# Gathers of a graph-attention kernel: leave to start at three instructions of a step instead of eleven

## The chip, the cores and the metric

The kernel runs on one core of one Trainium2 chip. The metric is the device time of one execution in microseconds (us), the median of several runs. Names of engines: PE is the TensorE (matmuls; PEld its weight loads), DVE the VectorE, ACT the ScalarE, POOL the GpSimd, SP the SyncE, which here only issues DMAs.

## The reference, cut to what matters

A graph layer with attention over 100,000 edges, 3,125 nodes, 5 edge types (relations) and 8 heads of 16 channels. The edges are sorted by destination.

```python
for r in range(5):
    mask = edge_types == r
    q = einsum('eh,khd->ekd', x[dst], W_Q[r])
    k = einsum('eh,khd->ekd', x[src], W_K[r])
    v = einsum('eh,khd->ekd', x[src], W_V[r])
    logits = (q * k).sum(-1) / 4 + attn_bias[r]
    # softmax over the edges of one destination and one relation
    attn = segment_softmax(where(mask, logits, -1e9), dst)
    out += segment_sum(attn * v, dst)
out = out @ out_proj_w.T + out_proj_b
h = layernorm(out + x) * gamma + beta
result = layernorm(x + h)
```

## The kernel before

**Tables first.** For every node and relation the kernel computes a row of keys and values (256 float32) and writes it to a table in device memory, `kv_d`; the queries go to a second table, `q_d`. This preamble takes about the first 105 us of the profile.

**Then steps.** The edges are taken 128 at a time (a tile), four tiles to a group and three groups to a step `k`, 66 steps in all (the first and the last have two groups). For each tile POOL issues one indirect DMA, a *gather* (L836), which fetches the 128 rows of `kv_d` that the tile's edges need. In 63 of the steps one of the twelve tiles is made by matmuls instead (`early_rows`, L1060, from rows of x gathered in the preamble at L371), so that a step has eleven gathers: 719 gathers at L836 in all, and 63 at L371.

**Where gathers land.** There are four slots of twelve tiles: three in the tile `kv_early`, one in `kv_late`; step `k` uses slot `k % 4` (`place`, L804). A gather may write a slot once the step that used it four steps earlier has been read for the last time, by `weigh` (L1118).

**One step.** DVE multiplies the gathered keys by the queries (`products`, L933), sums over channels (`logits`, L991), and adds the relation's mask (L966). PE turns the result (L1023). DVE then divides the sums of step `k-2` by their denominators (`norm`, L1169 its first instruction, L1173 its last), PE spreads the queries of step `k+1` (`spread_q`, L911, 36 matmuls into `qe`), DVE multiplies the values of step `k-1` by their weights (`weigh`, L1118), runs two scans that give the running maxima (L1073, L1077) and subtracts (L1087); ACT takes the exponential (L1095), PE turns it (L1102), and ACT copies the weights (`weights`, L1112), almost the last thing of the step. ACT also makes the matrices (L1131, L1135) by which PE sums edges into nodes (L1152, `sums`).

**What orders the gathers.** All engines run in the order in which the code writes their instructions; there is no scheduler. POOL's queue in the steps holds nothing but gathers. `gather(leave, n)` issues the next `n` of them and makes each wait for one instruction of another engine, its *leave* (`behind`, L154). `point(k, j, leave)` is called eleven times in a step, `j` from 0 to 10, and computes how many gathers should have been issued by then: those of the steps up to `k + (j+1)/11 + lead`, where `lead` falls evenly from 3.0 steps at the start (`KV_LEAD`) to 2.0 at the end (`KV_LOW`). As a step has about eleven gathers, each point issues about one. Besides its leave each gather waits for the landing of the gather eight places before it (eight semaphores, DMASW0 to DMASW7, are used in turn), and for whatever its slot needs, where the leave doesn't already cover that.

The points 6 to 10 of step `k-1` are written in the code of step `k`; the leaves of one round are, in the order of the code: `products(k)`, `weighted` (the L1112 copy of step `k-1`), `logits(k)`, the two ends of `norm(k-2)` (L1169, L1173), `weigh(k-1)` (L1118), `kept` (the last matmul of `spread_q(k+1)`, L911), the two scans (L1073, L1077), the masks `spot(k+2)` (L720) and `placed` (L1135).

Of the kernel before, what the change touches and what calls it, by code (L numbers as in the profile page):

```python
# [146 lines left out]
def windowed_path(  # L147
# [6 lines left out]
    def behind(gather, other):  # L154
        if other is not None:
            tc.add_manual_dep(
                gather.ins,
                other.ins.name,
                mybir.DependencyInfo(mybir.DependencyClass.Sync, mybir.DependencyReason.DATA),
                reason="leave",  # L160
            )
# [646 lines left out]
    def runs(a, b):  # L808
        out_ = []
        for q in range(a, b):  # L810
            k = AT[q // T][0]
            kv, at = place(k)
            at += q - T * G0[k]
            if out_ and out_[-1][0] is kv and out_[-1][2] == at:
                out_[-1][2] += 1
            else:
                out_.append([kv, at, at + 1])
        return out_
# [13 lines left out]
    def gather(leave=None, n=1):  # L832
        for q in sum(tiles, [])[len(issued) :][: max(n, 0)]:
            ((kv, at, _),) = runs(q, q + 1)
            behind(
                nc.gpsimd.indirect_dma_start(  # L836
                    out=kv[:, at, :], out_offset=None, in_=kv_d[:, :],
                    in_offset=bass.IndirectOffsetOnAxis(
                        ap=idx[:, q % T, q // T : q // T + 1], axis=0
                    ),  # L840
                ),
                leave,
            )
            issued.append(q)

    def point(k, j, leave):
        at = k + (j + 1) / POINTS
        at += KV_LEAD - (KV_LEAD - KV_LOW) * min(max(at / (NST - 3), 0.0), 1.0)
        whole = min(int(at), NST)
        n = sum(len(t) for t in tiles[:whole])  # L850
        if whole < NST:
            n += int((at - whole) * len(tiles[whole]) + 1e-6)
        gather(leave, n - len(issued))
# [493 lines left out]
    q_at = {k: b for b, k in q_from.items()}  # L1347

    gather(n=len(tiles[0]))
    assert len(marks) >= len(tiles[1]) + len(tiles[2])  # L1350
    for leave in marks[: len(tiles[1]) + len(tiles[2])]:
# [23 lines left out]
    for k in range(NST - 1):  # L1375
# [24 lines left out]
        if k < NST - 2:  # L1400
            point(k - 1, 6, products(k))
            point(k - 1, 7, weighted)
            point(k - 1, 8, logits(k))
            closed_lanes(k)
        else:
            places(G0[k])
            for g in range(G3 - 1):
                piece(k, g)
            made, summed = piece(k, G3 - 1)
            point(k - 1, 6, made)  # L1410
            point(k - 1, 7, weighted)
            point(k - 1, 8, summed)
# [642 lines left out]
```

## Time and profile before

| | before |
|---|---|
| time, median of 3 runs | 1020.38 us (1020.12 to 1023.06) |
| time of the profiled execution | 1029.88 us |
| span in that profile, first to last instruction | 1028.1 us |
| software DMA queue, which carries the gathers | 98.42 MB, 37.8% of the 16 DMA engines' span |
| mean granted TensorE clock | 0.961 |

The span is what the lines of the profile add up to; the profiled execution is 1.78 us longer than its span. A row of the timeline gives the start, the duration, the engine, the line of the code, the operation, what it writes and reads, and in brackets how long the engine had been idle and what ended that.

### The profile page before, as it was taken

Reading aid. Unit: us, or ns where it says so; the run is one execution under the profiler, and the core shown is the slowest. Engines: PE = TensorE matmul, PEld = TensorE weight load, DVE = VectorE, ACT = ScalarE, POOL = GpSimd, SP = SyncE. Lnnn points to the kernel's source line nnn. Section 1 sums busy time; section 2 is a strip of 40 time slices with the busy share of each in tenths; the row PEclk is TensorE's granted clock in tenths of the full one; section 3 lists DMA queues with packets and bytes.
Section 4 is the critical chain, followed back from the end, with each engine's and each line's share of the span. In section 5 each row is a group of like instructions: output and inputs, shape, how many; then the busy total and the mean of one; then the engine's idle time right before and its main releaser. Section 6 shows DMA issues by size and latency. Waiting matters only on the chain.

```text
span 1028.1 us, 21159 instructions
## 1 busy us (share of the span) xinstructions
PE 943.1 (92%) x6981; PEld 730.2 (71%) x6981; DVE 899.3 (87%) x1520; ACT 713.6 (69%) x1947; POOL 748.4 (73%) x793
## 2 busy tenths in 40 slices
PE   7995699999999999999999999999999999999896
PEld 3553578787777777777777777777777777777675
DVE  3665699899989998999999998999898999999895
ACT  2443368687777777777777777878777677877672
POOL 7777777777777777777777777777777777777730
PEclk9997599999999999999999999999999999999985
DMA  8997666666656666665666665666666566676620
GB/s 196 357 348 253 174 173 189 173 187 185 176 167 193 193 181 184 183 181 160 194 191 185 182 190 156 188 186 192 171 193 192 155 190 184 171 194 173 162 60 11
DMA packets 99077, 189.48 MB, mean 184 GB/s; under 512 B 19117, under 2 KB 59521, under 8 KB 98842
## 3 DMA queue, kind: packets, MB, share of 16 engines
q0 software_dynamic: 36528, 98.42, 37.8%
q1 hardware_dynamic: 61240, 88.74, 26.0%
q10 hardware_dynamic: 1194, 0.92, 0.4%
q8 instruction: 56, 0.92, 0.4%
q14 instruction: 59, 0.48, 0.2%
HBM read 157.61 MB, written 30.40 MB: 183 GB/s over the span
## 4 chain that ended last, share of the span: by engine, by line
DVE 35%; PE 26%; DMA 21%; issue 9%; ACT 4%; POOL 3%; DVEq 0%; ACTq 0%; SPq 0%; POOLq 0%
DMA kv_early<-kv_d,idx 14%; DVE qe L991 7%; PE both L1152 5%; DVE kv_early L933 5%; DMA kv_late<-kv_d,idx 5%; PE qe L911 4%; DVE wv L1118 4%; PE pr L508 3%; PE mid L1060 3%; POOL kv_early L836 3%; DVE run L1073 3%; DVE run L1077 3%; PE fin L1209 2%; DVE lx L966 2%; PE lt L1050 2%
## 5 line engine op out<-in xcount | busy, mean ns | idle before, releaser
L836 POOL DMA_INDIRECT kv_early<-kv_d,idx x543 | 515.9, 950 | 168.5 <-issue 85.9
L1152 PE MATMUL both<-wv,at 128*125 128x136 f32 x1552 | 269.4, 299 | 1.4 <-ACT at L1135 1.4
L1152 PEld LDWEIGHTS both<-wv,at 128*125 128x125 f32 x1552 | 207.9, 190 | 52.9 <-issue 46.0
L1131 ACT ACTIVATE at<-wide_at,nkey 128x125 f32<-128x125 f32 x776 | 245.0, 388 | 0.0
L836 POOL DMA_INDIRECT kv_late<-kv_d,idx x176 | 167.3, 950 | 53.6 <-issue 28.6
L1060 PE MATMUL mid<-wkv,xr 128*128 128x256 f32 x630 | 148.7, 383 | 1.6 <-ACT xr L1054 1.6
L911 PE MATMUL qe<-qw,hot 128*128 128x128 bf16 x2349 | 149.6, 225 | 0.0
L911 PEld LDWEIGHTS <-hot 128*128 128x128 bf16 x2352 | 145.4, 103 | 0.5 <-DVE vio L641 0.4
L1060 PEld LDWEIGHTS mid<-wkv,xr 128*128 128x128 f32 x630 | 116.4, 192 | 15.6 <-ACT xr L1054 2.0
L1135 ACT ACTIVATE at<-at 128x500 f32<-128x500 f32 x194 | 120.3, 620 | 6.1
L933 DVE TENSOR_TENSOR kv_early<-kv_early,qe 128x1536 f32<-128x1536 f32 (+3 forms) x70 | 89.2, 1275 | 25.9 <-DMA kv_early<-kv_d,idx 15.0
L1213 ACT COPY oT<-fin 128x25 f32 x194 | 35.1, 181 | 92.3 <-PE fin L1209 87.4
L1073 DVE TENSOR_TENSOR_SCAN run<-mk,lt 120x640 f32<-120x640 bf16 (+1 forms) x66 | 97.6, 1478 | 1.5 <-PE lt L1023 1.5
L1118 DVE TENSOR_TENSOR wv<-kv_early,mid 128x1536 f32<-128x1536 f32 (+2 forms) x51 | 86.2, 1692 | 12.4 <-PE mid L1060 9.3
L1077 DVE TENSOR_TENSOR_SCAN run<-lt,run 120x576 f32<-120x576 bf16 (+1 forms) x65 | 88.2, 1357 | 2.2
L991 DVE TENSOR_REDUCE qe<-kv_early 128x96 f32<-128x1536 f32 (+2 forms) x65 | 86.7, 1334 | 2.2
L1050 PE MATMUL lt<-diag,xg 128*128 128x512 f32 x252 | 84.1, 457 | 0.0
L1023 PE MATMUL lt<-ident,lx 128*120 128x128 f32 (+2 forms) x396 | 55.2, 277 | 26.8 <-DVE lx L966 10.7
L1023 PEld LDWEIGHTS lt<-ident,lx 128*120 128x120 f32 (+2 forms) x396 | 38.9, 137 | 55.7 <-ACT diag L1044 21.6
L1147 PE MATMUL both<-wv,over 128*5 128x136 f32 x386 | 77.3, 282 | 0.0
L1102 PEld LDWEIGHTS mid<-gather_heads,ls 120*128 120x128 f32 (+1 forms) x528 | 65.1, 194 | 15.0 <-ACT xTq L862 12.6
L1102 PE MATMUL mid<-gather_heads,ls 120*128 120x24 f32 (+1 forms) x528 | 67.4, 265 | 8.9 <-ACT xTq L862 7.5
(210 smaller groups left out, 1337.2 us busy)
## 6 DMA issues: line engine op xcount, KB each, us to landing
kt<-key_d SPq DMA_DIRECT2D x64, 384.0 KB
qw<-q_d SPq DMA_DIRECT2D x196, 96.0 KB
kv_d<-kvs SPq DMA_DIRECT2D x24, 640.0 KB
q_d<-q SPq DMA_DIRECT2D x25, 480.0 KB
mk<-msk_d SPq DMA_DIRECT2D x64, 150.5 KB
kv_early<-kv_d,idx POOLq DMA_INDIRECT x543
kv_late<-kv_d,idx POOLq DMA_INDIRECT x176
out<-z SPq DMA_DIRECT2D x24, 64.0 KB
```

Source lines behind the costliest of these rows:

```text
L836: nc.gpsimd.indirect_dma_start(out=kv[:, at, :], out_offset=None, in_=kv_d[:, :], in_offset=bass.IndirectOffsetOnAxis(ap=idx[:, q % T, q / ...
L911: spread = nc.tensor.matmul(dest[j], hot[:, j * P : (j + 1) * P], qw[:, c, :], start=(c == 0), stop=(c == 2),)
L933: made = nc.vector.tensor_tensor(kv[:, c0:c1, :H], kv[:, c0:c1, :H], qe[:, n:m], op=ALU.mult)
L991: made = nc.vector.tensor_reduce(lg[:, n : n + c1 - c0], heads(kv[:, c0:c1, :H]), AX.X, ALU.add)
L1060: nc.tensor.matmul(rows, xr[:, r * P : (r + 1) * P], wkv[:, r].rearrange("h s c -> h (s c)"), start=(r == 0), stop=(r == R - 1),)
L1073: there = nc.vector.tensor_tensor_scan(run[:n], mk[:n, 1 : WIDE + 1], lt, -BIG, op0=ALU.add, op1=ALU.max)
L1077: back = nc.vector.tensor_tensor_scan(run[:n, SEG:][:, ::-1], masks[:, SEG:][:, ::-1], run[:n, SEG:][:, ::-1], -BIG, op0=ALU.add, op1=ALU.max,
L1102: nc.tensor.matmul(ex.rearrange("p (i t) k -> p t i k", t=T)[:, t], ls[: n * LANES, t * P : (t + 1) * P], gather_heads[: n * LANES, :n], s ...
L1118: return nc.vector.tensor_tensor(heads(wv[:, a:b, :H]), heads(kv[:, at + a : at + b, H:]), ex[:, a:b, :, None].to_broadcast([P, b - a, HEA ...
L1131: nc.scalar.activation(at[:, t, :], row_at[:, :WR], AF.Abs, bias=nkey[:, t, g : g + 1], scale=1.0)
L1135: return nc.scalar.activation(at[:, :n], at[:, :n], AF.Relu, bias=1.0, scale=-1.0)
L1152: nc.tensor.matmul(pp[:WR], at[:, t, :], wv[:, T * i + t, :], start=(t == 0), stop=(t == end))
```

## The change

Only the points with `j` of 9, 1 and 7 issue anything; the count at such a point is computed as before, so it makes up for the points left out before it: in the order of the code six gathers at `j = 7`, two at `j = 9` and three at `j = 1` of a step of eleven. Their leaves are ACT's L1112 copy of the step before, DVE's L1169 and the last L911 matmul. Inside a batch only the first gather waits for the leave.

```diff
@@ def gather(leave=None, n=1):
                 ),
                 leave,
             )
+            leave = None
             issued.append(q)
 
     def point(k, j, leave):
+        if j not in (9,1,7,):
+            return
         at = k + (j + 1) / POINTS
         at += KV_LEAD - (KV_LEAD - KV_LOW) * min(max(at / (NST - 3), 0.0), 1.0)
```

The number and the order of the gathers stay the same, and so do all instructions of the other engines. What moves is the waits. POOL's queue about half-way, before (DMASW is the landing of an earlier gather; DVE, PE and Activation are the leaves or the freeing of a slot):

```order
L836 DMA kv_early<-kv_d,idx 128x256 [waits DMASW0_49,DVE_49]
L836 DMA kv_early<-kv_d,idx 128x256 [waits DMASW1_49,DVE_49]
L836 DMA kv_early<-kv_d,idx 128x256 [waits DMASW2_49,DVE_49]
L836 DMA kv_late<-kv_d,idx 128x256 [waits DMASW3_49,Activation_49]
L836 DMA kv_late<-kv_d,idx 128x256 [waits DMASW4_49,DVE_49]
L836 DMA kv_late<-kv_d,idx 128x256 [waits DMASW5_49,DVE_49]
L836 DMA kv_late<-kv_d,idx 128x256 [waits DMASW6_49,DVE_49]
L836 DMA kv_late<-kv_d,idx 128x256 [waits DMASW7_49,DVE_49]
L836 DMA kv_late<-kv_d,idx 128x256 [waits DMASW0_49,DVE_49]
L836 DMA kv_late<-kv_d,idx 128x256 [waits DMASW1_49,PE_49]
L836 DMA kv_late<-kv_d,idx 128x256 [waits DMASW2_49,DVE_49]
```

The same eleven gathers in POOL's queue of the changed kernel:

```order
L836 DMA kv_early<-kv_d,idx 128x256 [waits DMASW0_49,Activation_49]
L836 DMA kv_early<-kv_d,idx 128x256 [waits DMASW1_49]
L836 DMA kv_early<-kv_d,idx 128x256 [waits DMASW2_49]
L836 DMA kv_late<-kv_d,idx 128x256 [waits DMASW3_49,DVE_49]
L836 DMA kv_late<-kv_d,idx 128x256 [waits DMASW4_49]
L836 DMA kv_late<-kv_d,idx 128x256 [waits DMASW5_49,DVE_49]
L836 DMA kv_late<-kv_d,idx 128x256 [waits DMASW6_49]
L836 DMA kv_late<-kv_d,idx 128x256 [waits DMASW7_49,PE_49]
L836 DMA kv_late<-kv_d,idx 128x256 [waits DMASW0_49]
L836 DMA kv_late<-kv_d,idx 128x256 [waits DMASW1_49]
L836 DMA kv_late<-kv_d,idx 128x256 [waits DMASW2_49,Activation_49]
```

The first row's leave is now ACT's L1112 copy (it was DVE's scan L1073), the fourth row's wait is the freeing of the slot (it had been covered by a leave), the sixth waits for L1169, the eighth for L911, and with the eleventh the next batch begins. In the whole queue 707 of the 719 gathers waited for another engine besides their DMASW; in the changed kernel 249 do.

POOL's queue some five steps before the last gather, before:

```order
L836 DMA kv_late<-kv_d,idx 128x256 [waits DMASW7_49,DVE_49]
L836 DMA kv_late<-kv_d,idx 128x256 [waits DMASW0_49,DVE_49]
L836 DMA kv_late<-kv_d,idx 128x256 [waits DMASW1_49,DVE_49]
L836 DMA kv_early<-kv_d,idx 128x256 [waits DMASW2_49,DVE_49]
L836 DMA kv_early<-kv_d,idx 128x256 [waits DMASW3_49,PE_49]
L836 DMA kv_early<-kv_d,idx 128x256 [waits DMASW4_49,DVE_49]
```

and the same six gathers in the changed kernel:

```order
L836 DMA kv_late<-kv_d,idx 128x256 [waits DMASW7_49,DVE_49]
L836 DMA kv_late<-kv_d,idx 128x256 [waits DMASW0_49]
L836 DMA kv_late<-kv_d,idx 128x256 [waits DMASW1_49,PE_49]
L836 DMA kv_early<-kv_d,idx 128x256 [waits DMASW2_49]
L836 DMA kv_early<-kv_d,idx 128x256 [waits DMASW3_49]
L836 DMA kv_early<-kv_d,idx 128x256 [waits DMASW4_49,Activation_49]
```

In the third row the wait for PE's L911 stood two gathers later before, and in the sixth the wait for ACT's L1112 stood five gathers later: the same instructions of the other engines now hold back gathers that stand ahead of the ones that they held back.

## The prediction

> **What bounds the kernel now.** I read the busy times first, then POOL by stretches of 100 us, then POOL's timeline. From the page, part 1 and the groups of the gathers (busy time, mean of one, then the idle time before them and what ended it):
>
> ```profile
> PE 943.1 (92%) x6981; PEld 730.2 (71%) x6981; DVE 899.3 (87%) x1520; ACT 713.6 (69%) x1947; POOL 748.4 (73%) x793
> ...
> L836 POOL DMA_INDIRECT kv_early<-kv_d,idx x543 | 515.9, 950 | 168.5 <-issue 85.9
> ...
> L836 POOL DMA_INDIRECT kv_late<-kv_d,idx x176 | 167.3, 950 | 53.6 <-issue 28.6
> ```
>
> POOL looks least pressed of the big engines, at 73%. That is deceptive. Busy and idle of the gathers together are 515.9 + 168.5 + 167.3 + 53.6 = 905.3 us for 719 gathers, 1.26 us each, and the stretches say that this is the same everywhere (stretch, us, busy time, count):
>
> ```profile
> 100.00:200.00 100.00, 75.62 (x80) 0.86 0.65 176
> ...
> 800.00:900.00 100.00, 75.62 (x81) 0.98 0.64 176
> ```
>
> Eighty gathers in 100 us early, eighty-one late: one every 1.25 us, whatever the other engines do. The timeline of POOL at three places shows the spacing:
>
> ```profile
> 4.96 0.94 POOL L371 DMA_INDIRECT xg<-in_x,xf  x1 [0.30 <-issue]
> 6.21 0.95 POOL L371 DMA_INDIRECT xg<-in_x,xf  x1 [0.30 <-issue]
> ...
> 88.50 0.95 POOL L836 DMA_INDIRECT kv_early<-kv_d,idx  x1 [0.30 <-issue]
> 89.75 0.95 POOL L836 DMA_INDIRECT kv_early<-kv_d,idx  x1 [0.30 <-issue]
> ...
> 404.22 0.94 POOL L836 DMA_INDIRECT kv_late<-kv_d,idx  x1 [0.30 <-ACT ls L1095]
> 405.47 0.95 POOL L836 DMA_INDIRECT kv_late<-kv_d,idx  x1 [0.30 <-DVE mv L1250]
> ```
>
> 0.95 us of work and a fixed 0.30 us between two gathers. POOL has no free time from the first gather to the last, so **POOL is the bound**: a delay that makes it miss a place in this row isn't made up, because there is no slack in which to catch up. The names behind "<-" in the last two rows are whoever happened to finish then; an idle time of 0.30 us is no wait.
>
> **The wait that goes.** The three pairs differ in waits. The two gathers at 5 us wait for nothing, those at 88 us for a landing alone (DMASW), those at 404 us for a landing and a leave. All three are 1.25 us apart. So a wait that is already met costs POOL nothing, and removing 707 - 249 = 458 of them gains nothing. A view of line L836 shows what they are:
>
> ```profile
> L836 POOLq EVENT_SEMAPHORE  x711: 17/17/43, 83.7 to 988.1; - x178
> ```
>
> 17 ns each on POOL's sequencer, hidden behind the 0.95 us of the gather before. If they weren't hidden, 458 x 17 ns = 7.8 us would be gained. The two ends are thus -7.8 and 0; I take 0, since the equal spacing is the nearer row. The Trainium skill, "DMA: Bandwidth & Descriptors", section "Anatomy of one DMA — SWDGE (gpsimd) path", puts a dispatch by the sequencer at about 50 ns; charged for each removed wait, my estimate from that page would be 458 x 50 ns = 22.9 us less, a time of about 997.5 us, and the equal spacing at 5, 88 and 404 us speaks against it.
>
> **The waits that move: half-way.** Each batch's first gather now waits for an instruction that finishes later in the step than its old leave. What this costs depends on how far POOL runs behind its leaves. Rows of the timeline of ACT, DVE and POOL for the batch whose queue is shown above:
>
> ```profile
> 504.32 0.22 ACT L1112 COPY wv<-mid 128x96 f32<-128x96 f32 x1
> 506.56 0.18 DVE L1169 TENSOR_SCALAR both<-both 125x24 f32<-125x24 f32 x1
> 509.68 0.95 POOL L836 DMA_INDIRECT kv_early<-kv_d,idx  x1 [0.30 <-issue]
> 515.95 0.95 POOL L836 DMA_INDIRECT kv_late<-kv_d,idx  x1 [0.30 <-DVE stats L1249]
> ```
>
> The gather at 509.68 will wait for the copy that ended at 504.54, and the one at 515.95 for L1169, which ended at 506.74. Both leaves are over 5 us old when POOL gets there. Here the change does nothing. The waits for a free slot (L1118), which show in the new queue because no leave covers them any more, were met already in the old one, by leaves as old.
>
> **The waits that move: the end.** The lead in the code falls from 3 steps to 2, so POOL's lag behind its leaves shrinks. The last fifth decides. ACT's copies (the new leave of a batch of six) and the gathers that will wait for them:
>
> ```profile
> 808.83 0.22 ACT L1112 COPY wv<-mid 128x96 f32<-128x96 f32 x1
> 835.35 0.22 ACT L1112 COPY wv<-mid 128x96 f32<-128x96 f32 x1
> 876.74 0.22 ACT L1112 COPY wv<-mid 128x96 f32<-128x96 f32 x1
> 918.18 0.24 ACT L1112 COPY wv<-mid 128x96 f32<-128x96 f32 x1 [0.90 <-PE mid L1102]
> 956.92 0.22 ACT L1112 COPY wv<-mid 128x96 f32<-128x96 f32 x1
> 986.53 0.24 ACT L1112 COPY wv<-mid 128x96 f32<-128x96 f32 x1 [1.46 <-PE mid L1102]
> ...
> 807.98 0.94 POOL L836 DMA_INDIRECT kv_early<-kv_d,idx  x1 [0.30 <-issue]
> 834.26 0.95 POOL L836 DMA_INDIRECT kv_early<-kv_d,idx  x1 [0.30 <-issue]
> 875.62 0.95 POOL L836 DMA_INDIRECT kv_early<-kv_d,idx  x1 [0.30 <-issue]
> 915.66 0.95 POOL L836 DMA_INDIRECT kv_early<-kv_d,idx  x1 [0.30 <-issue]
> 957.03 0.95 POOL L836 DMA_INDIRECT kv_late<-kv_d,idx  x1 [0.30 <-issue]
> 982.04 0.95 POOL L836 DMA_INDIRECT kv_early<-kv_d,idx  x1 [0.30 <-DVE run L1077]
> ```
>
> Now the new leave ends after the gather's old start. Behind a gather that waits stand all later gathers, and DVE's products (L933) wait for these. How long a gather takes to start behind a leave that it really waits for is shown by the only two such waits of the old kernel, at its end (DVE, then POOL):
>
> ```profile
> 986.61 0.68 DVE L933 TENSOR_TENSOR kv_early<-kv_early,qe 128x512 f32<-128x512 f32 x1
> 996.24 0.54 DVE L933 TENSOR_TENSOR kv_early<-kv_early,qe 128x384 f32<-128x384 f32 x1
> ...
> 983.60 0.95 POOL L836 DMA_INDIRECT kv_early<-kv_d,idx  x1 [0.61 <-DVE hot L720]
> 987.56 0.95 POOL L836 DMA_INDIRECT kv_early<-kv_d,idx  x1 [3.01 <-DVE kv_early L933]
> 990.06 0.95 POOL L836 DMA_INDIRECT kv_early<-kv_d,idx  x1 [0.30 <-issue]
> ```
>
> L933 ended at 986.61 + 0.68 = 987.29, the gather began at 987.56: 0.27 us. With that, each shortfall is the end of the copy plus 0.27 less the old start: 1.34 us at 808, 1.58 at 834, 1.61 at 876, 3.03 at 916, 0.38 at 957 and 5.00 at 982 (986.77 + 0.27 - 982.04).
>
> **How they add.** If the leaves stayed where they were, the largest would count alone: 3.03 before the last step. If everything behind a stall moved with it, all would add: 12.9 us. Which it is depends on whether a step runs on gathers that have just landed. The chain of work that ended last shows three places where it does (start, us, what):
>
> ```profile
> 843.02 5.20 DMA kv_early<-kv_d,idx
> 848.39 1.62 DVE kv_early L933
> ...
> 899.39 3.63 DMA kv_late<-kv_d,idx
> 903.15 1.62 DVE kv_early L933
> ...
> 928.17 2.92 DMA kv_early<-kv_d,idx
> 931.10 1.77 DVE kv_early L933
> ```
>
> So I walk along. To 834 the stalls overlap and POOL is 1.58 us late. The product at 848.39 waits for the gather of 843.02, so from here the steps, and their leaves, are late by 1.58 too; at 876 POOL falls back to 1.58 + 1.61 = 3.19. The product at 903.15 hands that on; at 916 it is 3.19 + 3.03 = 6.22. The product at 931.10 hands it on; at 957 it is 6.60. In the last step the gather of 982.04 would be 6.60 + 5.00 = 11.60 late, but the old kernel's own waits there, 0.31 and 2.71 us beyond the usual 0.30, vanish inside it, so the last gather is 11.60 - 3.02 = 8.58 late and starts at 998.64. With a landing of 3.63 us as at 899 its rows are there at 1002.27; the product that uses them, at 996.24 before, stands at 1002.84 when all is 6.60 late. The last step adds nothing. **The sum is +6.6 us.**
>
> The edit touches no other engine's instructions, and POOL's spacing stays, so the DMA traffic stays as it is. The profiled execution took 1029.88 us, its span 1028.1; by the sum it becomes 1036.5. The median of the timed runs, 1020.38, is 9.5 us below the profiled time; I put the sum on it: **1027.0 us**.
>
> **Rivals.**
> - *All shortfalls add* (+12.9 us, 1033.3). For it: each stall makes more steps wait for their gathers, which then move their leaves. Against: only some products of the end stand directly behind a landing; in others DVE and PE work on without one.
> - *The leaves hold still* (at most +3.0 us, 1020.4 to 1023.4). For it: outside the three places the leaves come from PE, ACT and DVE work that no gather holds up. Were those engines somewhat quicker without the profiler, shortfalls of 1 to 3 us would shrink. Against: the chain's three places.
> - *The other side: the removed waits were in POOL's way after all.* If each of them took its 17 ns between two gathers, POOL, which is the bound, would finish 7.8 us sooner, at 1012.6 us. It decides as soon as a gather with one wait follows its neighbour by less than 1.25 us, from 88 us on; at about 1.24 us it would offset my stalls. Against it stand the equal spacings above.
> - *The edit doesn't take the waits away.* The slot's freeing comes back as a wait of its own on one gather of a step, which is why 249 are left and not three for each step, some 190. These are old when POOL reaches them, so the time is as in my forecast.
>
> **How the numbers follow.** Forecast (about 1024 to 1030): 0.60. All shortfalls add: 0.17. Leaves hold still: 0.15. Waits in POOL's way: 0.08. The first two are slower by over 0.3% (about what a measurement of this kernel can tell from no change, 3.1 us), together 0.77; the third is within it, 0.15; the last is faster, 0.08. The range runs from the time without a stall, 1020.4, to the full sum of the shortfalls, 1033.3, and leaves out the faster case and a little above.
>
> **What would show it.** In the profile after: POOL's spacing still 1.25 us with one wait and two; no idle time over 0.31 us on POOL before about 800 us; from there some six to ten idle times of 0.5 to 5 us ended by ACT L1112 or PE L911; the last gather near 998 us instead of 990. I would be wrong if the spacing fell, if POOL's stalls began in the first half (then the lag behind the leaves isn't what the rows half-way say), or if the stalls were there and the end didn't move.

## The result, and the profile after

The changed kernel takes 1028.20 us (median of 6 runs, 1026.16 to 1029.88); the kernel before took 1020.68 us beside it (6 runs, 1020.12 to 1023.96). The ratio is 1.006, with a 95% interval of 1.0042 to 1.0079: slower by 7.5 us. Here and below a ratio leaves out runs in a slower state, and it isn't exactly the quotient of the two medians.

The groups of the gathers in the profile after (columns as before):

```profile
L836 POOL DMA_INDIRECT kv_early<-kv_d,idx x543 | 515.3, 949 | 177.5 <-issue 131.7 <-DMA kv_early<-kv_d,idx 9.7 <-ACT wv L1115 9.0
L836 POOL DMA_INDIRECT kv_late<-kv_d,idx x176 | 167.1, 950 | 55.6 <-issue 43.6 <-PE qe L914 2.5 <-DMA kv_late<-kv_d,idx 1.2
```

Lines behind the edit have moved by three: L1112 is now L1115, L911 is L914, L933 is L936. Busy time is as it was. Idle time before the gathers was 168.5 + 53.6 = 222.1 us and is 177.5 + 55.6 = 233.1 us, 11.0 us more. The timeline of POOL shows where; these are all its idle times over 0.32 us from 300 us on (start, duration, then in brackets the idle time and what ended it):

```profile
807.60 0.94 POOL L836 DMA_INDIRECT kv_early<-kv_d,idx  x1 [1.22 <-ACT wv L1115]
834.21 0.94 POOL L836 DMA_INDIRECT kv_early<-kv_d,idx  x1 [0.66 <-ACT wv L1115]
876.44 0.95 POOL L836 DMA_INDIRECT kv_early<-kv_d,idx  x1 [1.24 <-ACT wv L1115]
914.60 0.94 POOL L836 DMA_INDIRECT kv_late<-kv_d,idx  x1 [2.23 <-PE qe L914]
919.22 0.94 POOL L836 DMA_INDIRECT kv_early<-kv_d,idx  x1 [1.17 <-ACT wv L1115]
945.81 0.94 POOL L836 DMA_INDIRECT kv_early<-kv_d,idx  x1 [2.94 <-PE qe L914]
949.83 0.94 POOL L836 DMA_INDIRECT kv_early<-kv_d,idx  x1 [0.58 <-ACT wv L1115]
963.60 0.94 POOL L836 DMA_INDIRECT kv_late<-kv_d,idx  x1 [0.33 <-ACT wv L1115]
977.49 0.94 POOL L836 DMA_INDIRECT kv_early<-kv_d,idx  x1 [0.43 <-ACT wv L1115]
992.11 0.94 POOL L836 DMA_INDIRECT kv_early<-kv_d,idx  x1 [3.68 <-ACT wv L1115]
999.65 0.94 POOL L836 DMA_INDIRECT kv_early<-kv_d,idx  x1 [2.85 <-PE qe L914]
```

Nothing before 800 us, then eleven stalls, eight behind ACT's copy and three behind PE's last matmul. Beyond the usual 0.30 us they add up to 14.0 us; the 3.0 us of the old kernel's own two waits at its end are gone, and 11.0 us are left. From the timeline of DVE, the last product, which stood at 996.24 us:

```profile
1002.89 0.55 DVE L936 TENSOR_TENSOR kv_early<-kv_early,qe 128x384 f32<-128x384 f32 x1 [0.15 <-DMA kv_early<-kv_d,idx]
```

It is 6.65 us later. Yet the two spans are equal, 1028.1 us. The stretches of both kernels behind the last product say why (stretch, us, busy time of PE, PEld, DVE, ACT, POOL with counts, then the granted TensorE clock, DMA share, GB/s). Before:

```profile
997.00:1010.00 13.00, 12.73 (x55) 10.12 (x56) 9.56 (x22) 9.20 (x27) 0.00 (x0) 0.54 0.01 2
1010.00:1028.10 18.10, 9.54 (x37) 6.76 (x36) 9.16 (x38) 2.02 (x9) 0.00 (x0) 0.50 0.05 15
```

After:

```profile
997.00:1010.00 13.00, 11.50 (x88) 9.59 (x88) 12.50 (x18) 10.91 (x34) 0.94 (x1) 0.90 0.08 22
1010.00:1028.10 18.10, 8.38 (x54) 5.91 (x52) 12.20 (x49) 5.10 (x15) 0.00 (x0) 0.78 0.05 16
```

In the profiled execution of the kernel before, the clock fell to 0.54 and 0.50 in the last 30 us, where PE does the work: from the start of the last product to the end it took 1028.1 - 996.24 = 31.9 us. In that of the changed kernel, at 0.90 and 0.78, it took 25.2 us. In the other profiles on a chip where the kernel before takes 1022 us this stretch took 25.2 to 25.9 us. The kernel before itself, profiled a second time (on another chip, below), took 25.2 us, at 1.00 in the first 13 us behind the start of the last product and 0.72 in the rest; the first profile, cut in the same way, has 0.57 and 0.50. So the old profile has some 6.7 us in its tail that go with its clock and not with the kernel, and the spans can't be compared; the positions up to the last product can, and they agree with the timed runs.

### The profile page after: what moved, and what is told of

Its sections match the earlier page's. It is cut to its first block, busy times and chain, and to the rows that moved or that the text cites. A ratio compares the mean times of both kernels' runs of the same rounds, so it can differ in the third digit from the quotient of the medians.

```text
span 1028.1 us, 20701 instructions
## 1 busy us (share of the span) xinstructions
PE 938.9 (91%) x6981; PEld 728.9 (71%) x6981; DVE 900.6 (88%) x1520; ACT 713.9 (69%) x1947; POOL 746.9 (73%) x793
## 4 chain that ended last, share of the span: by engine, by line
PE 33%; DVE 27%; DMA 16%; POOL 11%; issue 10%; ACT 3%; ACTq 0%; DVEq 0%; POOLq 0%
DMA kv_early<-kv_d,idx 12%; POOL kv_early L836 8%; PE both L1155 7%; DVE qe L994 6%; PE qe L914 5%; DVE kv_early L936 4%; PE pr L508 4%; PE mid L1063 4%; DMA kv_late<-kv_d,idx 3%; POOL kv_late L836 3%; PE fin L1212 3%; PE lt L1053 2%; PE mid L1105 2%; DVE run L1076 2%; DVE kv_late L936 2%
## 5 line engine op out<-in xcount | busy, mean ns | idle before, releaser
L836 POOL DMA_INDIRECT kv_early<-kv_d,idx x543 | 515.3, 949 | 177.5 <-issue 131.7
L1155 PE MATMUL both<-wv,at 128*125 128x136 f32 x1552 | 266.2, 296 | 0.6 <-ACT at L1138 0.6
L1155 PEld LDWEIGHTS both<-wv,at 128*125 128x125 f32 x1552 | 205.7, 188 | 51.2 <-issue 45.1
L836 POOL DMA_INDIRECT kv_late<-kv_d,idx x176 | 167.1, 950 | 55.6 <-issue 43.6
L914 PE MATMUL qe<-qw,hot 128*128 128x128 bf16 x2349 | 153.5, 228 | 0.0
L914 PEld LDWEIGHTS <-hot 128*128 128x128 bf16 x2352 | 148.7, 105 | 0.5 <-DVE vio L641 0.4
L936 DVE TENSOR_TENSOR kv_early<-kv_early,qe 128x1536 f32<-128x1536 f32 (+3 forms) x70 | 89.2, 1276 | 32.7 <-DMA kv_early<-kv_d,idx 22.3
L1026 PE MATMUL lt<-ident,lx 128*120 128x128 f32 (+2 forms) x396 | 55.6, 279 | 33.0 <-DVE lx L969 17.7
L1053 PE MATMUL lt<-diag,xg 128*128 128x512 f32 x252 | 84.7, 459 | 0.0
```

The lines of the kernel that those rows point to most:

```text
L836: nc.gpsimd.indirect_dma_start(out=kv[:, at, :], out_offset=None, in_=kv_d[:, :], in_offset=bass.IndirectOffsetOnAxis(ap=idx[:, q % T, q / ...
L914: spread = nc.tensor.matmul(dest[j], hot[:, j * P : (j + 1) * P], qw[:, c, :], start=(c == 0), stop=(c == 2),)
L936: made = nc.vector.tensor_tensor(kv[:, c0:c1, :H], kv[:, c0:c1, :H], qe[:, n:m], op=ALU.mult)
L1026: nc.tensor.transpose(live["lt", k][: n * LANES, c : c + w], live["lx", k][p : p + w, j : j + n].rearrange("p g r k -> p (g r k)"), ident[ ...
L1053: nc.tensor.matmul(lt[:, c0:c1], xg[:, e, :], at[:, c0:c1], start=True, stop=True)
L1155: nc.tensor.matmul(pp[:WR], at[:, t, :], wv[:, T * i + t, :], start=(t == 0), stop=(t == end))
```

## The experiments

Theory A is that of the prediction: gathers go out every 1.25 us whatever they wait for, and only the leaves that come late behind 800 us cost. Rival C: the eleven leaves spread the gathers over a step, and that is worth something in itself, anywhere in the program.

The chips differed. On one the kernel before took 1022.02 us; on the two others it took 1301.77 and 1302.42 us, with the same instructions. Each result is therefore compared with the kernel before on its own chip. The four runs on the chip of 1022 us come first.

**The changed kernel again.** No edit.

> The changed kernel itself, beside the kernel before on the same chip. Theory A (the gathers are issued every 1.25 us whatever they wait for, and only the leaves that come too late after 800 us cost): on a chip where the kernel before takes about 1021 us the ratio is 1.006 to 1.009 (+6 to +9 us), with POOL idle times of 0.4 to 3.7 us ended by ACT's copy L1115 or PE's L914 behind 800 us and none before. Rival C (leaves spread the gathers, and three of eleven spread them worse): on a chip where the kernel before takes about 1302 us, where the kernel with three leaves and a wait at each gather took 1.070, the ratio is 1.05 to 1.09 and PE's results reach ACT and DVE late all through the span. If rival C is at work on the first kind of chip too, stalls of ACT or DVE behind finished PE work are in the profile before 800 us there.

1028.87 us, ratio 1.0058 (1.0034 to 1.0081). POOL's stalls are of the same kind: ten from 808.91 us on, nine of them behind L1115 or L914 and one, 1.53 us idle at 919.30, that the trace puts down to a landing. Two more come early: 1.66 us idle at 725.98 behind ACT's L1115 and 0.49 at 752.54 behind ACT's L885. "None before 800 us" was a miss, then; the rest is theory A's. Of late work behind finished PE work there is no sign: each of the 63 copies that take PE's L1053 result starts 0.04 us after the matmul or after ACT's preceding instruction.

**Three leaves in the late steps only.**

```diff
-        if j not in (9,1,7,):
+        if k >= 52 and j not in (9,1,7,):
```

> Eleven leaves up to step 51, three from step 52 on; one waiting gather per batch throughout. Theory A, where the kernel before takes about 1021 us: all of the cost of the change is in the steps from 52 on, so the ratio is that of the changed kernel (1.006 to 1.009), and the last gather starts near 999 us as in the changed kernel. Rival C: the cost is spread over the 64 steps, so about a fifth of the changed kernel's loss is left (about 1.001 on that kind of chip, 1.01 to 1.02 where the kernel before takes about 1302 us).

1028.22 us, ratio 1.0059 (1.0035 to 1.0084): all of the loss, with a fifth of the edit. From the waits of POOL in this kernel (who waited for whom, us in total, times, longest):

```profile
POOL kv_early L836 <- ACT wv L1115: 10.5, 8, 4.3
POOL kv_early L836 <- PE qe L914: 5.8, 10, 1.8
```

The last gather starts at 997.33 us and the last product at 1001.34, in the changed kernel's second profile at 997.33 and 1001.35. The loss is made behind step 52, as theory A says.

**Three leaves in the early steps only.**

```diff
-        if j not in (9,1,7,):
+        if k < 52 and j not in (9,1,7,):
```

> Three leaves up to step 51, eleven from step 52 on; one waiting gather per batch throughout. Theory A, where the kernel before takes about 1021 us: the late leaves are gone, only the one or two near 808 and 834 us stay, and they cost 0 to 2 us: 1.000 to 1.002, last gather near 990 to 991 us. Rival C: four fifths of the changed kernel's loss stay (about 1.005; 1.04 to 1.07 where the kernel before takes about 1302 us).

1022.53 us, ratio 0.9993 (0.9969 to 1.0018): no loss that can be told from none. Rival C's 1.005 lies outside the interval. Groups of the gathers in this kernel:

```profile
L836 POOL DMA_INDIRECT kv_early<-kv_d,idx x543 | 515.1, 949 | 168.8 <-issue 124.9 <-DMA kv_early<-kv_d,idx 9.4 <-DVE run L1080 4.0
L836 POOL DMA_INDIRECT kv_late<-kv_d,idx x176 | 167.0, 949 | 53.6 <-issue 43.0 <-DMA kv_late<-kv_d,idx 2.4 <-DMA kv_early<-kv_d,idx 1.2
```

The end of POOL's timeline in the same kernel:

```profile
981.47 0.95 POOL L836 DMA_INDIRECT kv_early<-kv_d,idx  x1 [0.60 <-DVE hot L720]
985.43 0.94 POOL L836 DMA_INDIRECT kv_early<-kv_d,idx  x1 [3.01 <-DVE kv_early L936]
986.68 0.94 POOL L836 DMA_INDIRECT kv_early<-kv_d,idx  x1 [0.30 <-DVE both L1172]
987.93 0.94 POOL L836 DMA_INDIRECT kv_early<-kv_d,idx  x1 [0.30 <-issue]
```

This kernel is also the test of the removed waits. In its queue 337 of the 719 gathers wait for another engine besides their DMASW, against 707 before: 370 waits are gone, and late leaves take next to nothing back: the stalls that were expected near 808 and 834 us are not there, but two come at 724.23 and 750.79, 0.48 and 0.49 us idle, so 0.4 us beyond the usual 0.30. The idle time before the gathers is 168.8 + 53.6 = 222.4 us, against 222.1. At 17 ns each they would have saved 6.3 us; the interval allows at most 3.2. The two waits at the end are the old kernel's, 0.60 and 3.01 us.

**Three leaves, a larger lead at the end.**

```diff
-KV_LOW = 2.0
+KV_LOW = 3.0
```

> The changed kernel with a lead that stays at 3.0 steps to the end and doesn't fall to 2.0 (KV_LOW 3.0). Theory A, where the kernel before takes about 1021 us: each late leave is then a step's length older than the gather that waits for it, no late leave is left, the last gather starts at or before 990 us, and the ratio is 0.996 to 1.002. A rival, that slots and not leaves hold the late gathers (DVE's L1121 has to free them): the gathers wait for DVE then, and the ratio stays at 1.003 to 1.009. Where the kernel before takes about 1302 us this kernel took 1.073 and should again.

1021.93 us, ratio 0.9988 (0.9968 to 1.0008). The same three leaves, a step older: no idle time over 0.32 us on POOL is left behind 300 us. The last rows of POOL and of the products in its timeline:

```profile
984.50 0.95 POOL L836 DMA_INDIRECT kv_early<-kv_d,idx  x1 [0.30 <-DVE kv_early L936]
985.75 0.95 POOL L836 DMA_INDIRECT kv_early<-kv_d,idx  x1 [0.30 <-issue]
...
993.28 0.68 DVE L936 TENSOR_TENSOR kv_early<-kv_early,qe 128x512 f32<-128x512 f32 x1
994.96 0.54 DVE L936 TENSOR_TENSOR kv_early<-kv_early,qe 128x384 f32<-128x384 f32 x1
```

The age of the leaves is thus the cause: make them older, and the loss is gone. The rival that slots hold the late gathers falls, since POOL doesn't wait for DVE there. The rows show a limit too. In the kernel with three leaves in the early steps, which ends with the old leaves on the same chip, the last gather started at 987.93 us and the last product at 994.12. Here the last gather is 2.2 us earlier, yet the last product 0.8 us later, and it starts with no idle time before it. In the last step DVE's own queue is then late next, so a yet earlier gather buys nothing. This kernel ties with the one before; no kernel here beats it.

**The other chips.** The remaining eight ran on the two chips of 1302 us. First the kernel before itself, with no edit:

> The kernel before, profiled a second time. In its first profile the TensorE clock granted in the last 31 us was 0.54 and 0.50, and those 31.9 us after the last product were 6.7 us longer than in the changed kernel's profile. If that clock is what hid the loss between the two profiled executions, a second profile with a clock near 0.8 or more there has the last product again near 996 us and a span near 1021 us; if the tail of this kernel is long by itself, the span is near 1028 us again. Ratio 1.000 by every theory.

1305.39 us, ratio 1.0025 (0.9986 to 1.0064). On this chip neither 996 nor 1021 us can come out, but the stretch behind the last product answers the question: 25.2 us at 1.00 and 0.72, so this kernel's tail isn't long by itself. Then each half of the change alone. Three leaves, with a wait at every gather of a batch (the changed kernel without this line):

```diff
-            leave = None
             issued.append(q)
```

> The three points of the changed kernel, but every gather of a batch waits for the leave again. Theory A (the loss is the late place of the leaves, a wait that is met costs nothing): the same stalls as in the changed kernel, +7 us, ratio 1.006 to 1.007. Rival B (the removed waits save POOL time, and the stalls cost more than is seen): slower than the changed kernel by up to 458 x 17 ns = 8 us more, ratio up to 1.014. Rival C (the loss comes from gathers that start without a leave and crowd the DMA): no loss, ratio 1.000.

> Three leaves a step, and every gather of a batch waits for its leave, not only the first. Where the kernel before takes about 1021 us: theory A (a met wait costs POOL nothing, all the loss is in the later leaves) gives the changed kernel's time, ratio 1.004 to 1.008, median spacing 1.25 us, last gather at 997 to 1000 us. A rival, that the waits which the change takes away were worth up to 17 ns each and so hid part of the loss, gives up to 1.5 us more for each hundred, and 1.009 to 1.014. Where the kernel before takes about 1302 us: 1.07 as before.

Ratios 1.0702 (1.0642 to 1.0761) and 1.0692 (1.0640 to 1.0744), on one chip each. And eleven leaves, with a wait at the first gather of a point only (the kernel before with this line):

```diff
+            leave = None
             issued.append(q)
```

> The kernel before with only the second part of the change: leaves at all eleven points, and only the first gather of a point's batch waits. Theory A: a point issues one or two gathers, so few waits go, and none of them was in POOL's way: 0.998 to 1.002, spacing 1.25 us, last gather at 987 to 991 us, as before. The rival of waits in POOL's way: under 0.998.

1302.36 us, ratio 0.9955 (0.9911 to 0.9998). Both edits turned out to be none: with `leave = None` taken out of the changed kernel, the instructions of every engine and their waits are the same as with it, 249 of 719 gathers waiting; with it put into the kernel before, they are the same as in that kernel, 707. A second wait for a leave that POOL has already waited for isn't in the queue in the first place. So the half of the change that drops it does nothing, and the batches alone took the waits from 707 to 249; the rival that put 17 ns on each dropped wait had nothing to act on. It also means two things for the numbers: the changed kernel's own ratio on these chips is 1.07, and 0.9955 is what no change can look like here.

Without any leave (`gather(leave, ...)` of the kernel before becomes `gather(None, ...)`):

```diff
-        gather(leave, n - len(issued))
+        gather(None, n - len(issued))
```

> All gathers of the steps without any leave; they wait for their slot and for the landing eight gathers back alone. Theory A: POOL's spacing stays 1.25 us, the two waits at the end of the old kernel (3.0 us together) go, the last gather lands 3 us sooner, but its product stands 2.5 us behind that already: -0 to -1 us, ratio 0.999 to 1.000. Rival B (waits cost POOL time): -7.8 us or more, ratio 0.992 or less. Rival C (crowding without leaves): slower, ratio over 1.006.

> The kernel before without any leave: a gather starts as soon as its slot is free and POOL is. Where the kernel before takes about 1021 us, theory A (POOL's 1.25 us a gather is the bound, a leave can only hold it up): no POOL idle time of a leave is left, gathers run ahead until slots stop them (idle times ended by DVE's L1118), the last one starts 3 us or more before 990 us, and the ratio is 0.994 to 1.002. Rival C (leaves spread the gathers, and without them bursts of gathers delay what ACT and DVE get from PE): over 1.02, with ACT and DVE waiting for long finished PE work, as where the kernel before takes about 1302 us (1.34 there).

1748.07 us (1.3416, 1.3341 to 1.3490) and 1746.42 us (1.3458, 1.3383 to 1.3533). Last, three leaves with larger leads, `KV_LOW` 3.0 and 2.5:

> The changed kernel with a lead of 3.0 steps to the end (KV_LOW 3.0 instead of 2.0), so that each leave near the end is the one of a step earlier. Theory A: no POOL idle time over 0.31 us anywhere after the preamble, the loss is gone, ratio 0.999 to 1.000. If batching as such costs (C), or if three leaves are too few at any lead, it stays at 1.006.

> The changed kernel with a lead that falls from 3.0 to 2.5 steps and not to 2.0. Theory A: half a step is about 6 us, more than any of the shortfalls, so nearly all late leaves are gone: at most 0.5 to 2 us of POOL idle time for leaves behind 800 us, last gather at 987 to 991 us, ratio 0.998 to 1.002. If the loss went with the lead in proportion (half of it back): 1.002 to 1.004 and a last gather near 993 us. Where the kernel before takes about 1302 us: 1.07.

Ratios 1.0730 (1.0670 to 1.0789) and 1.0708 (1.0660 to 1.0756): the lead, which cured the loss on the chip of 1022 us, does nothing here. On a chip of 1022 us neither the lead of 2.5 nor the kernel without leaves was run, so what they do there is open. Theory A's numbers for the edited kernels fail on these chips; they hold where POOL's row of gathers is the bound, and here it isn't. Rival C's do hold: the fewer leaves, the longer the time, 1 with eleven, 1.07 with three, 1.34 with none. What goes on is seen in rows of the kernel before on such a chip (PE, ACT and POOL, from its timeline):

```profile
500.21 1.33 PE L1050 MATMUL lt<-diag,xg 128*128 128x512 f32 x4
500.83 0.95 POOL L836 DMA_INDIRECT kv_late<-kv_d,idx  x1 [0.30 <-issue]
...
503.34 0.95 POOL L836 DMA_INDIRECT kv_late<-kv_d,idx  x1 [0.30 <-issue]
504.29 0.69 ACT L1054 COPY xr<-lt 128x640 f32<-128x640 f32 x1 [3.10 <-PE both L1152]
```

and in rows of the kernel without leaves:

```profile
848.67 0.95 POOL L836 DMA_INDIRECT kv_late<-kv_d,idx  x1 [9.29 <-DVE wv L1118]
...
852.83 0.27 PE L857 MATMUL mid<-ident,xn 128*128 128x128 f32 x1
...
861.17 0.95 POOL L836 DMA_INDIRECT kv_late<-kv_d,idx  x1 [0.30 <-issue]
864.47 0.27 ACT L862 COPY xTq<-mid 128x128 f32<-128x128 f32 x1 [11.84 <-remote]
```

PE's L1050 ended at 501.54, and the copy that takes its result started at 504.29, 2.75 us later. In the second, PE's transpose ended at 853.10 in the middle of eleven gathers back to back, and ACT's copy, which had been idle for 11.84 us, started at 864.47, 2.35 us after the last of them (861.17 + 0.95 = 862.12). "Remote" means that the trace has no instruction near enough that could have released it. The view of line L1054 in the profile of before that the prediction read (what ended ACT's idle time ahead of it, us, times):

```profile
  PE lt L1050: 22.5, 51
```

The same view of the same kernel on a chip of 1302 us:

```profile
  remote: 54.9, 21
  PE both L1152: 12.2, 9
  issue: 10.2, 7
  PE lt L1050: 2.5, 3
```

In these two kernels ACT and DVE thus take up PE's results late while gathers run back to back. How late a copy starts, counted from the end of PE's matmul or of its own engine's preceding instruction, whichever came later, differs by line. With eleven leaves it is 2.0 us on average for L1112, 1.1 for L1054 and 1.7 for DVE's L1169; without leaves it is 9.3 us for L862 and 6.1 for L873, but nothing for L1054. With three leaves this isn't the whole story: L862, L1054, L1112 and L1169 (lines named as in the kernel before) start within 0.05 us there, only the copies of L1213 are late, by 0.6 us on average and up to 9.1, and much of the loss stands on PE itself. Its L911 matmuls in the profile of before that the prediction read, and the same matmuls with three leaves on a chip of 1302 us (the run with a wait at every gather):

```profile
L911 PE MATMUL qe<-qw,hot 128*128 128x128 bf16 x2349 | 149.6, 225 | 0.0
L913 PE MATMUL qe<-qw,hot 128*128 128x128 bf16 x2349 | 178.4, 222 | 151.3 <-issue 141.6
```

PE is idle for 151.3 us before them, and for 141.6 of these the trace shows nothing that it waited for. Nearly all of it, 149.9 us, is in 174 pauses of up to 2.2 us between two of these matmuls, inside their batch of 36; in the kernels on the chip of 1022 us there is no such pause. A gather runs in 54% of the paused time and in 49% of the whole span, so the pauses alone don't point at the gathers.

The granted clock falls too, to 0.898 with eleven leaves, 0.844 with three and 0.774 with none, from 0.961, and PE's busy time grows from 943 us to 1030, 1115 and 1110; whether the lower clock is a part of the cause or comes of the waiting is not shown.

Gathers that follow one another by less than 1.4 us form runs of 3.4 on average with eleven leaves (719 gathers in 211 runs), 5.4 with three (132) and 10.9 with none (66), in the order of the three times. That the runs have a part in the delay is likely by this order and by the rows. Long runs alone don't do it: in the profile of before that the prediction read, all 719 gathers stand in four runs, and none of these copies is late. Through what the runs delay PE's work is not shown, nor why one chip has it and another not.

## Why the prediction was right, step by step

- **The time.** 1027.0 us was forecast, 1028.2 measured; the sum of +6.6 stands against +7.5 in the first comparison and +6.9 in the second (1028.87 - 1022.02). Right, on chips of the first kind. The range and the chances knew nothing of a chip where the change costs 7%.
- **POOL's fixed 1.25 us, the removed waits worth nothing.** Right: spacing is 1.25 us in both profiles, and the kernel with three leaves in the early steps took away 370 waits for nothing.
- **Half-way nothing happens, the loss begins near 800 us.** Right, by the kernels with three leaves early and late.
- **The shortfalls.** Mis-sized, in two directions. The sum had six stalls behind ACT's copy, 12.9 us together; measured, beyond the usual 0.30, the eight are 0.92, 0.36, 0.94, 0.87, 0.28, 0.03, 0.13 and 3.38, 6.9 us. It had none behind PE's last L911 matmul, the leave of the batch of three, though that was named among the signs to look for; there are three, 1.93, 2.64 and 2.55, 7.1 us. The copy of 918 us was to hold POOL for 3.03 us and did so for 0.87, because PE's leave had already held it for 1.93 five microseconds before. A leave that comes late is seldom alone: I should have worked out each of the three leaves of each late step. Up to 957 us, the part that counts, the sum had 6.60 us, all from ACT's copies; measured are 3.4 us from these and 4.6 from PE's matmul. That the total came so near is luck: the copies' excess and PE's missing terms cancel in great part.
- **How the stalls add.** Right in kind, wrong in place, and the agreement to 0.1 us is again luck. The last gather moved from 990.06 to 999.65 us (+9.6, forecast +8.6), and the last product by 6.65 (forecast 6.6); the last step's stalls added nothing to the product, as said. But of the three products that should hand the delay on, the chain of the changed kernel shows (start, us, what):

```profile
842.98 4.27 DMA kv_early<-kv_d,idx
847.43 1.62 DVE kv_early L936
...
900.19 3.43 DMA kv_late<-kv_d,idx
903.68 1.62 DVE kv_early L936
...
931.90 3.04 DMA kv_early<-kv_d,idx
934.96 1.77 DVE kv_early L936
```

  They stood at 848.39, 903.15 and 931.10. The first two are 1.0 us earlier and 0.5 later, where the walk had 1.6 and 3.2 later; the changed profile was about 1.3 us ahead when it reached 800 us, which takes a part of that, and the rest is the smaller stalls. The third is 3.9 us later. The rest of the delay comes in at a place that the walk doesn't have, the next step's product (before, then after):

```profile
943.51 1.75 DVE L933 TENSOR_TENSOR kv_early<-kv_early,qe 128x1536 f32<-128x1536 f32 x1 [1.12 <-ACT at L1131]
949.71 1.75 DVE L936 TENSOR_TENSOR kv_early<-kv_early,qe 128x1536 f32<-128x1536 f32 x1 [3.26 <-DMA kv_early<-kv_d,idx]
```

  In the kernel before it waited for no landing; in the changed one it waits for a gather behind the stall of 2.94 us at 945.81, and is 6.2 us late. From there to the end the products are 6.2 to 6.7 us late. The old chain of work also has landings ahead of the products of 862.88 and 957.54, which the prediction left out; they change nothing in its sum. Counted from the 1.3 us that the changed profile was ahead, the loss is nearer to 7.9 us, which is also what POOL's stalls up to 950 us add up to; on one chip, the changed kernel against the one with three leaves in the early steps, the last product is 7.2 us later (1001.35 against 994.12).
- **"The profiled execution becomes 1036.5."** Wrong: it took 1029.88, as before. The sum was put on a profile whose last 30 us ran at a clock of 0.54 and 0.50; the changed kernel's did not. The profiled time lay 9.5 us above the median, and that tail is most of it; it should have been seen as such, and the forecast put on the median alone.
- **Rivals.** "All shortfalls add" (+12.9) and "leaves hold still" (3.0 at most) are both outside the measured 6.9 to 7.5. "Waits in POOL's way" falls with the 370 waits. "The edit doesn't take the waits away" is half true in a way that I hadn't seen: its second line takes none.

## What to carry to other kernels

A wait that was already met cost nothing on this queue, where gathers follow one another by a fixed 1.25 us; before waits are removed, look at the spacing of instructions with none, one and two of them, and see whether the doubled waits are in the queue at all. Batching waits moves each one to a later event, which costs just where the queue's lag behind its events is shorter than the step between them: work out that slack for every wait of the last, thinnest stretch, not for one kind of them, and where it is negative, issue the work further ahead, as the lead of 3.0 did here. A schedule that costs 0.6% on one chip may cost 7% on another, for a reason that wasn't found, so a ratio belongs to the chip that it was measured on.

## What the runs showed of the hardware that was not expected

Two of the chips run the same program in 1302 us instead of 1021, with every gather still 0.95 us (947 ns on average for L836 there, 950 in the profile of before) and 1.25 us apart inside a run. Instructions of ACT and DVE take as long as before (L1131 389 ns against 388, L1118 1699 against 1692); of PE's, L1060 takes 523 ns on average against 383, at the lower granted clock. The way from PE's results to ACT and DVE is slow in places: 0.04 us for each of the 63 copies of L1054 in the profile of before that the prediction read, 1.1 us on average and up to 5.1 on a chip of 1302 us, and up to 11.8 us for the copies of L862 in the kernel without leaves, in the midst of or right behind back-to-back gathers. The trace also holds fewer semaphore updates there, 8,395 against 22,421 for the kernel before, and nearly all that are missing tell of landings of DMAs (5,415 against 18,494), so the names of what ended a wait are less sure on these chips. The cause was not found.

The stretch behind the last product came in two lengths, whatever the kernel and the chip: 31.9 us in three of the fourteen profiles, with a granted clock of 0.57 in its first 13 us and 0.50 in the rest, and 25.2 to 26.6 us in the other eleven, with 0.74 to 1.00 and 0.64 to 0.77.
